# Two wide units for the last image's depthwise conv, and edge zeros stored one by one

## The chip, the core and the metric

The kernel runs on one core of a Trainium2 chip. The metric is the device time of one launch in microseconds; the time given is the median of three runs, and one further execution was taken with a profile. The engines are TensorE (PE, with its weight loads as PEld), VectorE (DVE), ScalarE (ACT), GpSimd (POOL) and SyncE (SP); SP, ACT and POOL also issue DMA transfers.

## What is computed

Input is x of 4 images, 128 channels, 128 x 128 pixels, all f32. Two layers follow each other. The first is a transformer-like block on overlapping 16 x 16 regions and the second a quantised residual block:

```
reg  = 9 x 9 regions of 16 x 16 pixels, step 14          # per image
y    = layernorm(tok); q, k, v = split(y @ w_qkv)        # 4 heads of 32
tok  = softmax(q k^T / sqrt(32)) v @ w_out + b_out + tok
xf   = overlapping regions added, divided by their count
y    = layernorm(xf) @ w_p0 + b_p0                       # 256 channels
ym   = depthwise 5 x 5 conv of y, padding 2, channel by channel
ym   = batchnorm over all images and pixels
x1   = gelu(gelu(ym)) @ w_p2 + b_p2 + xf

out  = conv3x3(act_quant(x1), weight_quant(w1)) -> batchnorm
out  = conv3x3(act_quant(out), weight_quant(w2)) -> batchnorm
result = out + x1
```

The batch norm after the depthwise conv needs the mean and variance of every channel over all four images. Nothing of the gelu stage can be computed before the last image's depthwise conv is done.

## The kernel before

**Bands.** The first layer goes through 36 bands, `bands[t] = (image, row of regions)`, nine a image. Band t has nine regions j = 0 to 8. For each region the loop at L1014 to L1027 issues the scores, the values of the region before, and four lists of side steps, which `beside(t)` (L917) lays out: the layer norm and q, k projections of later bands (`a1`, `a2`, from `ln1_chunks`), and for band t-1 the output projection, layer norm and the projection to 256 channels (`b1`, `b2`, from `post_chunks`). Of the eleven steps of a `b` chunk, 0 and 1 are the output projection, 2 to 6 the layer norm, and 7 to 10 the p0 projections, whose results `y` are stored to `y2_d` in DRAM. PE, ACT, DVE and SP execute in the order in which the code issues; POOL's order is the scheduler's.

**The depthwise conv.** It reads `y2_d` back with rows on the partitions: 16 output rows need 20 input rows of even and odd pixels, so 40 partitions. A group is 16 rows of an image, eight groups an image. Weights are banded matrices `dw_d`, made on the chip at the start. A unit, `units` at L170, is (image, first group, number of groups). One conv piece takes 8 channels of each of two halves; its matmuls (`depthwise`, L614) have 40 rows, 32 columns and 64 pixels x groups of moving columns. Images 0 to 2 are one unit of eight groups each; the last image is cut in three units of 4, 2 and 2 groups.

`conv_steps(n)` (L637) makes a list of steps for a unit: a begin that loads two tiles ahead, and then for each tile a step that loads the tile two ahead, does the matmuls into a `pm` bank, copies them with ACT to `c`, takes `bn_stats` with DVE, and puts the stores of `c` to `cv_d` in the list `stores`. `run` (L980) issues after each step the stores that were waiting before it. For the last image a tile has 640 KB of input in runs of 2 KB, 240 KB of weights, and 512 KB of results in runs of 256 bytes.

**When they run.** `todo` holds the waiting conv steps, `share` over how many bands they are spread. In `beside` (L925 to L935) an image's unit is queued two bands after its last band; for the last image the unit of four groups is queued in band 33 and spread over two bands, and the second unit goes into band 35 alone, with two pieces at a region (`twice`, lists `c` and `d`). A band takes `n` steps (L938) at the regions named at L953.

**The tail.** After the last band the pool context `bctx` is closed, with the conv's buffers `up` and `cp`. `conv_rest` (L715) opens new ones for the third unit: it loads all its weights with POOL (L609) and some input rows with SP at once; then the last band's projections run (`beside(T)`, L943 to L947); then `rest()` loads the missing rows and does eight steps of 16 channels, two groups wide, into the banks of the scores (`sc`), with `chunk_stats` after each. Then follow the batch norm (from L1097) and the gelu stage.

**The start.** The padding of `y2_d` must be zero. `band_matrices` (L213) makes a list of steps that also goes through `todo`, ten bands long: `zeros`, four steps `edges(b)` (for images 0 to 2 three stores of 256, 896 and 896 KB each from one zero tile, for the last image two of 256 KB), `padded_taps`, sixteen steps `by_outputs`, and the turning of the weights. For the bands up to 9 the lists are laid out anew at L973 to L977.

Of the kernel before, what the change touches and what calls it, by code (L numbers as in the profile page):

```python
# [8 lines left out]
F32 = mybir.dt.float32  # L9
# [5 lines left out]
P = 128  # L15
# [4 lines left out]
NR = (P - RS) // STEP + 1  # L20
NT = RS * RS
# [10 lines left out]
GR = 16  # L32
CW = P // 2
KD = 2 * (GR + 4)
NCK = 8
NG = P // GR + 1
# [12 lines left out]
def layers(  # L49
# [120 lines left out]
    units = [(b, 0, P // GR) for b in range(B - 1)] + [(B - 1, g, n) for g, n in ((0, 4), (4, 2), (6, 2))]  # L170
# [14 lines left out]
    with ExitStack() as actx:  # L185
# [7 lines left out]
        small = pool("small", 6)  # L193
        ps_s, ps_o, ps_m = (pool(n, k, space=PSUM) for n, k in (("ps_s", 1), ("ps_o", 1), ("ps_m", 3)))
# [5 lines left out]
        up, cp = pool("up", 3), pool("cp", 3)  # L200
# [12 lines left out]
        def band_matrices():  # L213
# [18 lines left out]
            def edges(b):  # L232
                if b == B - 1:
                    for d in (y2_d[b][0:2], y2_d[b][P + 2 :]):
                        nc.sync.dma_start(
                            out=d.rearrange("r e c x -> (r e c x)").rearrange("(p n) -> p n", p=P),
                            in_=held["zero"][:, : 8 * CW],
                        )
                    return
                for m, n, g in ((0, 8, 0), (4, 28, NG - 1), (18, 28, NG - 1)):  # L240
                    nc.sync.dma_start(
                        out=bass.AP(
                            y2_d[b].tensor, y2_d[b][m, 0, g, 0:1].offset,
                            [[n * NG * CW, P], [NG * CW, n], [1, CW]],
                        ),
                        in_=held["zero"][:, : n * CW].rearrange("p (n x) -> p n x", x=CW),
                    )

# [48 lines left out]
            steps = [zeros, *each(edges, [(b,) for b in range(B)]), padded_taps, lambda: None]  # L297
            steps += each(by_outputs, [(ro,) for ro in range(GR)])
# [338 lines left out]
        def conv_steps(n, ahead=2):  # L637
# [39 lines left out]
            def products(at):  # L677
                k, jj, c0 = tiles[at]
                ut, wt = U.pop(at), W[k, jj]
                pc = [ps_m.tile([P, nj, ng, CW], F32, name="pm") for _ in range(2)]  # L680
                depthwise(pc, wt[:, :, c0:], ut, nc_)
                for half in range(2):
                    cv = cp.tile([P, nj, ng, CW], F32, name="c")
                    nc.scalar.copy(  # L684
                        cv.rearrange("p j g x -> p (j g x)"), pc[half].rearrange("p j g x -> p (j g x)")
                    )
                    for j in range(nj):
                        nc.vector.bn_stats(  # L688
                            st0[:, k, half, 2 * jj + c0 // 4 + j, n, :], cv[:, j].rearrange("p g x -> p (g x)")
                        )  # L690
                        ch = 32 * k + 16 * half + 8 * jj + c0 + 4 * j
                        store(
                            bass.AP(
                                cv_d[b].tensor,
                                cv_d[b][g0, ch, 0:1].offset,
                                [[CW, P], [2 * P * GR * P, ng], [1, CW]],
                            ),
                            cv[:, j],
                        )
# [6 lines left out]
            for at in range(len(tiles)):  # L706
                def one(at=at):
                    if at + ahead < len(tiles):
                        load(at + ahead)
                    products(at)  # L710

                steps.append(one)
            return steps

        def conv_rest(n, w_t, u_t, c_t):  # L715

            b, g0, ng = units[n]
            early = 3  # L720
            at = GR + 2

            def load(k, a, z, g, m):
                for half in range(2):
                    ch = 32 * k + 16 * half
                    nc.sync.dma_start(
                        out=U[k][64 * half + 2 * a : 64 * half + 2 * z, g : g + m].rearrange(
                            "p g c x -> p g (c x)"
                        ),
                        in_=input_of(b, g0 + g, m, ch, 16, a, z),  # L730
                    )

            U = [u_t.tile([P, ng, 16, CW], F32, name=f"u{k}") for k in range(NCK)]
            W = [w_t.tile([P, 3, 16, 32], F32, name=f"w{k}") for k in range(NCK)]
            for k in range(NCK):
                weights(W[k], k, 0, 2, nc.gpsimd.dma_start)
            for k in range(early):
                load(k, 0, at, 0, 1)

            def late(k):  # L740
                if k < early:
                    load(k, 0, at, 1, 1)
                    load(k, at, GR + 4, 0, ng)
                else:
                    load(k, 0, GR, 0, ng)
                    load(k, GR, GR + 4, 0, ng)

            def step(k):
                sc = ps_s.tile([P, 2, 2, NT], F32, name=f"sc{k % 2}")
                pc = [  # L750
                    sc[:, half].rearrange("p a n -> p (a n)").rearrange("p (j g x) -> p j g x", j=4, g=ng)
                    for half in range(2)
                ]
                depthwise(pc, W[k], U[k], 16)
                for half in range(2):
                    cv = c_t.tile([P, 4, ng, CW], F32, name=f"c{half}")
                    nc.scalar.copy(
                        cv.rearrange("p j g x -> p (j g x)"), pc[half].rearrange("p j g x -> p (j g x)")
                    )
                    for j in range(4):  # L760
                        nc.vector.bn_stats(
                            st0[:, k, half, j, n, :], cv[:, j].rearrange("p g x -> p (g x)")
                        )
                    engine = (nc.sync, nc.scalar)[half]
                    for g in range(ng):
                        engine.dma_start(
                            out=bass.AP(
                                cv_d[b].tensor,
                                cv_d[b][g0 + g, 32 * k + 16 * half, 0:1].offset,
                                [[CW, P], [4 * GR * P, 4], [1, CW]],  # L770
                            ),
                            in_=cv[:, :, g],
                        )

            def run_all():
                for k in range(4):
                    late(k)
                for k in range(NCK):
                    step(k)
                    chunk_stats(k)  # L780
                    if k + 4 < NCK:
                        late(k + 4)

            return run_all
# [132 lines left out]
        def beside(t, sel=None):  # L917
# [7 lines left out]
            if t >= 2:  # L925
                b, i = bands[t - 2]
                if i == NR - 1 and b < B - 1:
                    todo.extend(conv_steps(b))
                    share[0] = NR if b < B - 2 else 5
                elif b == B - 1 and i == 4:  # L930
                    todo.extend(conv_steps(B - 1))
                    share[0] = 2
                elif b == B - 1 and i == 6:
                    todo.extend(conv_steps(B))
                    share[0] = 1  # L935
# [3 lines left out]
            conv = [todo.pop(0) for _ in range(n)]  # L939
# [3 lines left out]
            if t == T:  # L943
                return [
                    *conv, *left, *b1[:2], *b2[:2], b1[2], b1[3], b2[2], b2[3], b1[4], b2[4], b1[5], b2[5],
                    b1[6], *b1[7:], b2[6], *b2[7:],
                ]  # L947
# [3 lines left out]
            d = [[] for _ in range(NR)]  # L951
            twice = len(conv) > NR
            for j in sorted((1, 3, 5, 7, 8, 4, 6, 2, 0)[: len(conv)]):  # L953
                c[j] = [conv.pop(0)]
                d[j] = [conv.pop(0)] if twice and j and conv else []
# [17 lines left out]
            if t <= NR:  # L973

                left[:] = [*b1[9:], *b2[7:]]
                full = (f[:3], f[3:], b1[:2], a1[5:7], a1[7:], b2[:2], a2[5:7], a2[7:], b1[7:9])
                plan = [(one, two, w, four) for (one, two, three, four), w in zip(plan, full)]  # L977
            return [(one, two, three, four + d[j]) for j, (one, two, three, four) in enumerate(plan)]
# [9 lines left out]
        todo, share, left, early = [], [0], [], []  # L988
# [14 lines left out]
        with nullcontext() if safe else tc.manual_schedule(engines=MANUAL):  # L1003
# [25 lines left out]
            assert not todo  # L1029
# [4 lines left out]
            pools = [actx.enter_context(tc.tile_pool(name=f"late{n}_{tag}", bufs=n)) for n in (1, 2)]  # L1034
# [3 lines left out]
            rest = conv_rest(len(units) - 1, pools[0], pools[0], pools[1])  # L1038
            run(beside(T, selector(pools[0].tile([P, 4 * P], F32, name="sel"))))
# [403 lines left out]
```

## Time and profile before

| what | us |
|---|---|
| median of 3 runs (3217.94 to 3236.64) | 3229.64 |
| the profiled execution | 3224.37 |
| its span, first to last instruction | 3222.6 |
| PE busy in it (94%) | 3034.8 |
| DVE busy (63%) | 2018.5 |
| ACT busy (62%) | 1983.9 |
| POOL busy (26%) | 841.0 |

The bands begin, by the first matmul of their scores, at these times of the span:

| stretch | us of the span | length, us |
|---|---|---|
| band 2 | 117.0 to 178.0 | 61.0 |
| bands 3 to 8, each | from 178.0 | 47.6 to 48.5 |
| band 10, the first with conv | 514.8 to 581.5 | 66.7 |
| bands 20 to 26, each | from 1092.1 | 56.1 to 58.1 |
| bands 28 to 32, each | from 1547.8 | 68.5 to 73.2 |
| bands 33, 34, 35 | 1899.2 to 2193.3 | 84.2, 96.2, 113.7 |
| tail up to the batch norm's first matmul | 2193.3 to 2286.2 | 92.9 |

The page cuts the span in 40 slices of 80.6 us; a digit is the busy share in tenths, and PEclk the clock that TensorE was granted:

```profile
PE   8989998999999999999899998876899999999998
PEclk9999999999999999999999999977799999999999
GB/s 89 147 198 164 180 180 184 192 219 207 212 218 165 200 209 216 201 213 193 172 227 235 225 190 202 200 167 197 278 357 354 361 359 298 158 165 77 119 357 308
```

The columns 25 to 28 hold bands 33 to 35 and the tail. From column 29 on the gelu stage and the two 3 x 3 convs run, with PE above 90%.

The queues of the page, by packets, MB and share of the time of 16 DMA engines: q1 is issued by SP, q10 by ACT, q0 by POOL.

```profile
q1 hardware_dynamic: 763311, 645.37, 71.9%
q10 hardware_dynamic: 15712, 37.02, 4.4%
q0 software_dynamic: 1024, 3.93, 0.4%
```

### The profile page before, as it was taken

How to read it: one execution, taken by the hardware profiler on the slowest of the kernel's cores; microseconds unless marked ns; L12 is line 12 of the kernel's file. 1: busy time of each engine (PE TensorE's matmuls, PEld its weight loads, DVE VectorE, ACT ScalarE, POOL GpSimd, SP SyncE). 2: the span in 40 equal slices, each digit the busy share in tenths (PEclk: the TensorE clock that was granted, in tenths of full speed). 3: DMA queues.
4: the chain of work that ended last, by engine and by line, in shares of the span. 5: the costliest groups of instructions: out<-in, count | busy, mean ns of one | idle time of the engine just before them, and what ended most of it. 6: DMA issues, size and time to landing. Idle time of an engine off the chain costs nothing.

```text
span 3222.6 us, 92155 instructions
## 1 busy us (share of the span) xinstructions
PE 3034.8 (94%) x39162; PEld 1471.6 (46%) x39162; DVE 2018.5 (63%) x3244; ACT 1983.9 (62%) x2658; POOL 841.0 (26%) x1058
## 2 busy tenths in 40 slices
PE   8989998999999999999899998876899999999998
PEld 4545544444444444444444444454544444444443
DVE  5767886777776677767566654543555555666543
ACT  5767776777777777777666654532477777433433
POOL 3434443333333333333233231211111111000000
PEclk9999999999999999999999999977799999999999
DMA  3575777798886888887799978867899999442398
GB/s 89 147 198 164 180 180 184 192 219 207 212 218 165 200 209 216 201 213 193 172 227 235 225 190 202 200 167 197 278 357 354 361 359 298 158 165 77 119 357 308
DMA packets 780468, 692.32 MB, mean 215 GB/s; under 512 B 606022, under 2 KB 659599, under 8 KB 772367
## 3 DMA queue, kind: packets, MB, share of 16 engines
q1 hardware_dynamic: 763311, 645.37, 71.9%
q10 hardware_dynamic: 15712, 37.02, 4.4%
q8 instruction: 311, 5.10, 0.7%
q0 software_dynamic: 1024, 3.93, 0.4%
q14 instruction: 110, 0.90, 0.1%
HBM read 414.61 MB, written 275.51 MB: 214 GB/s over the span
## 4 chain that ended last, share of the span: by engine, by line
PE 73%; DMA 10%; ACT 6%; issue 4%; DVE 3%; SPq 3%; ACTq 0%; POOL 0%; DVEq 0%; POOLq 0%
PE pc L1200 21%; PE pm L448 16%; PE sc L820 8%; PE po L883 8%; PE pm L623 7%; PE pb L1264 6%; PE po L891 3%; DMA cv_d<-c 3%; PE pm L387 3%; ACT pt L828 2%; DMA y_d<-y 2%; DMA w<-dw_d 2%; DVE rd L903 1%; DMA xn<-row 1%; DMA row<-rstd 1%
## 5 line engine op out<-in xcount | busy, mean ns | idle before, releaser
L903 DVE RECIPROCAL rd<-po 128x256 f32<-128x256 f32 x324 | 568.6, 1755 | 372.7 <-PE po L891 371.7
L1200 PE MATMUL pc<-q,wq 128*128 128x512 fp8e4 x3168 | 699.4, 380 | 5.1 <-DVE q L1212 5.1
L828 ACT ACTIVATE pt<-sc 128x1024 f32<-128x1024 f32 x648 | 628.1, 1025 | 112.3 <-PE sc L820 55.1
L838 POOL TENSOR_TENSOR sm<-pt 128x512 f32<-128x512 f32 x324 | 415.4, 1282 | 1040.2 <-ACT pt L828 791.2
L1200 PEld LDWEIGHTS <-wq 128*128 128x128 fp8e4 x3168 | 308.8, 98 | 406.0 <-issue 37.3
L820 PE MATMUL sc<-q,kr 32*128 32x256 f32 x5184 | 402.3, 408 | 22.2 <-ACT pt L828 20.1
L623 PE MATMUL pm<-u,w 40*32 40x504 f32 (+5 forms) x7680 | 358.0, 497 | 27.1 <-DMA u<-y_d 16.9
L883 PE MATMUL po<-pt,v 128*32 128x256 f32 x5184 | 359.7, 395 | 17.3 <-DVE part L907 14.6
L820 PEld LDWEIGHTS sc<-q,kr 32*128 32x128 f32 x5184 | 248.0, 186 | 276.6 <-issue 177.6
L684 ACT COPY c<-pm 128x512 f32<-128x512 f32 (+1 forms) x256 | 133.7, 563 | 312.0 <-PE pm L623 177.7
L688 DVE BATCH_NORM_STATS2 st<-c 128x6 f32<-128x512 f32 (+2 forms) x320 | 162.5, 551 | 210.9 <-ACT c L684 210.8
L838 DVE TENSOR_TENSOR sm<-pt 128x512 f32<-128x512 f32 x324 | 245.0, 756 | 29.6 <-ACT pt L828 29.5
L448 PE MATMUL pm<-xn,wp 128*32 128x512 f32 (+1 forms) x2304 | 244.0, 549 | 17.3 <-ACT y L577 8.5
L448 PE MATMUL pm<-xn,wqkv 128*32 128x512 f32 (+1 forms) x2304 | 247.1, 551 | 7.7 <-ACT v L811 5.5
L577 ACT ACTIVATE y<-pm,vectors 128x512 f32<-128x512 f32 (+1 forms) x288 | 183.0, 643 | 106.9 <-DMA y_d<-y 53.2
L1264 PE MATMUL pb<-cv,wp 128*128 128x512 f32 x512 | 233.3, 599 | 4.7 <-ACT cv L1255 4.6
L623 PEld LDWEIGHTS pm<-u,w 40*32 40x32 f32 x7680 | 143.4, 111 | 202.3 <-issue 144.2
L883 PEld LDWEIGHTS po<-pt,v 128*32 128x32 f32 x5184 | 139.2, 111 | 187.4 <-issue 103.2
L1208 DVE BATCH_NORM_STATS2 st<-pc 128x6 f32<-128x512 f32 x256 | 165.8, 690 | 83.7 <-PE pc L1200 83.7
L891 PE MATMUL po<-sm,ones 128*32 128x256 f32 x2592 | 206.9, 388 | 0.1
L910 POOL TENSOR_TENSOR ob<-ob,part 128x32 f32<-128x32 f32 x288 | 127.3, 442 | 237.8 <-DVE part L907 230.2
L448 PE MATMUL pm<-wqkv,yr 128*32 128x128 f32 x5184 | 179.8, 278 | 0.0
(157 smaller groups left out, 3400.5 us busy)
## 6 DMA issues: line engine op xcount, KB each, us to landing
cv<-cv_d SPq DMA_DIRECT2D x64, 1024.0 KB
cv_d<-c SPq DMA_DIRECT2D x192, 256.0 KB
xn<-row SPq DMA_DIRECT2D x76, 512.0 KB
y_d<-y SPq DMA_DIRECT2D x142, 256.0 KB
xfl<-xf_d SPq DMA_DIRECT2D x64, 512.0 KB
id_d<-y SPq DMA_DIRECT2D x64, 512.0 KB
idt<-id_d SPq DMA_DIRECT2D x64, 512.0 KB
out_dram<-z SPq DMA_DIRECT2D x64, 512.0 KB
```

The lines of the kernel that those rows point to most:

```text
L448: nc.tensor.matmul(out[m], w[:, m], v, start=True, stop=True)
L577: nc.scalar.activation(y[:, :n], pm[:, : n * P].rearrange("p (r c e) -> p r e c", r=n, e=2), AF.Identity, bias=bp0[:, h : h + 1],)
L623: nc.tensor.matmul(outs[half][32 * q : 32 * q + 32, j, :, a:z], wt[hs, s, c, :], ut[hs, :, c, a + s - 1 : z + s - 1], start=(s == 1), stop ...
L820: nc.tensor.matmul(sc[h // 2][:, h % 2, kc, :].rearrange("p (r c) -> p r c", c=RS), region(kr, j)[hs, kc * P : (kc + 1) * P], queries(j, h ...
L828: nc.scalar.activation(pt, sc[p], AF.Exp)
L838: add(sm, pt[:, :, 0, :], pt[:, :, 1, :], ALU.add)
L883: nc.tensor.matmul(po[hs, 0, :], v[:, kc, hs], pt[h // 2][:, h % 2, kc, :], start=(kc == 0), stop=(kc == 1),)
L891: nc.tensor.matmul(po[hs, 1, :], ones, sm[h // 2][:, h % 2, :], start=True, stop=True)
L903: nc.vector.reciprocal(rd, po[:, 1, :])
L1200: nc.tensor.matmul(pc[:, h], w[:, t, :], q1[b][:, r + dy : r + dy + RB, dx : dx + P], start=(t == 0), stop=(t == 8),)
L1208: nc.vector.bn_stats(st[:, 2 * n + h, :], pc[:, h])
L1264: nc.tensor.matmul(pb[:, m], wp2[:, h, :], cv[:, h, px], start=(h == 0), stop=(h == 1))
```

## The change

The last image's conv is cut in two units of four groups. The first is queued in band 33 as before, but `share` is 7: bands 33, 34 and 35 take 2, 3 and 3 of its 17 steps, and what is left runs in the tail between the steps of the last projections. There it uses the score banks, and its copies, statistics and stores (`results`) come at the next piece (`pending`). `conv_rest` does the second unit in 16 pieces of 8 channels, with a ring of six inputs and weights; one half of each input is loaded by SP, the other by POOL. `up` and `cp` stay open in the tail.

The edge zeros become eleven single steps, one beside each of the first eleven `by_outputs`. The regions at which conv steps stand are chosen in another order when a list is fresh, and in the bands up to 9 the output projection of `b2` comes two regions earlier.

```diff
-    units = [(b, 0, P // GR) for b in range(B - 1)] + [(B - 1, g, n) for g, n in ((0, 4), (4, 2), (6, 2))]
+    units = [(b, 0, P // GR) for b in range(B - 1)] + [(B - 1, 0, 4), (B - 1, 4, 4)]
...
-            steps = [zeros, *each(edges, [(b,) for b in range(B)]), padded_taps, lambda: None]
-            steps += each(by_outputs, [(ro,) for ro in range(GR)])
+            steps = [zeros, padded_taps, lambda: None]
+            edges = [(b, m, n, g) for b in range(B - 1) for m, n, g in ((0, 8, 0), (4, 28, NG - 1), (18, 28, NG - 1))]
+            edges += [(B - 1, 0, 8, 0), (B - 1, 0, 8, 1)]
+            for ro in range(GR):
+                steps.append(several(*each(edge, edges[ro : ro + 1]), lambda ro=ro: by_outputs(ro)))
...
             def products(at):
                 k, jj, c0 = tiles[at]
                 ut, wt = U.pop(at), W[k, jj]
-                pc = [ps_m.tile([P, nj, ng, CW], F32, name="pm") for _ in range(2)]
+                if tail:
+                    pc = score_banks(at, ng)
+                else:
+                    pc = [ps_m.tile([P, nj, ng, CW], F32, name="pm") for _ in range(2)]
                 depthwise(pc, wt[:, :, c0:], ut, nc_)
+                return pc
...
                     if at + ahead < len(tiles):
                         load(at + ahead)
-                    products(at)
+                    while pending:
+                        pending.pop(0)()
+                    pc = products(at)
+                    if tail:
+                        pending.append(lambda: results(at, pc))
+                    else:
+                        results(at, pc)
...
+            tiles = [(k, jj) for k in range(NCK) for jj in range(2)]
+            ahead = 6
...
+            def load(at, a, z, g, m):
+                k, jj = tiles[at]
+                for half, engine in enumerate((nc.sync, nc.gpsimd)):
+                    engine.dma_start(
+                        out=U[at][64 * half + 2 * a : 64 * half + 2 * z, g : g + m].rearrange(
                             "p g c x -> p g (c x)"
                         ),
+                        in_=input_of(b, g0 + g, m, 32 * k + 16 * half + 8 * jj, 8, a, z),
                     )
...
+            for at in range(ahead):
+                begin(at)
+                load(at, 0, GR, 0, ng - 1)
+                load(at, GR, GR + 4, 0, ng - 2)
...
             def run_all():
+                for at in range(ahead):
+                    load(at, 0, GR, ng - 1, 1)
+                    load(at, GR, GR + 4, ng - 2, 2)
+                for at in range(len(tiles)):
+                    step(at)
+                    if at % 2:
+                        chunk_stats(at // 2)
+                    if at + ahead < len(tiles):
+                        begin(at + ahead)
+                        load(at + ahead, 0, GR, 0, ng)
+                        load(at + ahead, GR, GR + 4, 0, ng)
...
                     todo.extend(conv_steps(B - 1))
-                    share[0] = 2
-                elif b == B - 1 and i == 6:
-                    todo.extend(conv_steps(B))
-                    share[0] = 1
+                    share[0] = 7
...
             if t == T:
+                more = lambda n: [todo.pop(0) for _ in range(min(n, len(todo)))]
                 return [
-                    *conv, *left, *b1[:2], *b2[:2], b1[2], b1[3], b2[2], b2[3], b1[4], b2[4], b1[5], b2[5],
-                    b1[6], *b1[7:], b2[6], *b2[7:],
+                    *more(2), *b1[:2], *b2[:2], b1[2], *more(1), b1[3], b2[2], *more(1), b2[3], b1[4], b2[4],
+                    *more(1), b1[5], b2[5], *more(1), b1[6], *b1[7:], b2[6], *more(1), *b2[7:], *more(len(todo)),
                 ]
...
-            for j in sorted((1, 3, 5, 7, 8, 4, 6, 2, 0)[: len(conv)]):
+            order = (1, 5, 7, 3, 8, 4, 6, 2, 0) if fresh else (1, 5, 3, 7, 8, 4, 6, 2, 0)
+            for j in sorted(order[: len(conv)]):
...
-                full = (f[:3], f[3:], b1[:2], a1[5:7], a1[7:], b2[:2], a2[5:7], a2[7:], b1[7:9])
+                full = (f[:3], f[3:], b1[:2], b2[:2], a1[5:7], a1[7:], a2[5:7], a2[7:], b1[7:9])
...
             run(left)
             left.clear()
             flush(len(stores))
-            rest = conv_rest(len(units) - 1, pools[0], pools[0], pools[1])
-            run(beside(T, selector(pools[0].tile([P, 4 * P], F32, name="sel"))))
+            rest = conv_rest(len(units) - 1, late)
+            run(beside(T, selector(late.tile([P, 4 * P], F32, name="sel"))))
+            run(pending)
             flush(len(stores))
             rest()
```

## The prediction

> **What bounds the kernel now.** I read the windows by stage first, cut where a band's first scores start. Columns: stretch, its length, busy time of PE, weight loads, DVE, ACT, POOL with counts, granted clock, DMA share, GB/s.
>
> ```profile
> core 0: us, PE busy (x) PEld busy (x) DVE busy (x) ACT busy (x) POOL busy (x), PEclk, DMA share, GB/s
> ...
> 1092.10:1490.20 398.10, 392.79 (x6396) 185.67 (x6392) 283.40 (x440) 289.70 (x439) 147.12 (x186) 1.00 0.87 209
> 1899.20:1983.40 84.20, 73.08 (x1408) 39.41 (x1400) 45.65 (x81) 44.72 (x69) 21.11 (x27) 0.92 0.81 186
> 1983.40:2079.60 96.20, 79.91 (x1600) 43.54 (x1592) 48.68 (x91) 46.66 (x73) 19.90 (x24) 0.93 0.87 204
> 2079.60:2193.30 113.70, 88.14 (x2232) 54.37 (x2224) 48.46 (x116) 42.19 (x77) 17.26 (x20) 0.82 0.65 171
> 2193.30:2233.80 40.50, 20.07 (x144) 7.19 (x144) 8.22 (x15) 10.00 (x17) 10.12 (x20) 0.79 0.86 231
> 2233.80:2286.20 52.40, 43.27 (x1536) 39.73 (x1537) 26.02 (x133) 8.59 (x16) 0.00 (x0) 0.50 0.69 166
> 2338.00:2528.00 190.00, 190.00 (x675) 84.75 (x674) 104.24 (x156) 134.15 (x105) 27.07 (x26) 1.00 0.99 358
> ```
>
> Bands 20 to 26 (the first row) are bound by PE: 393 of 398 us at full clock, 57 us a band. Bands 33, 34, 35 take 84, 96 and 114 us for the same attention, with gaps on PE and a clock below one. The tail is 40.5 us up to the first matmul of `conv_rest` and 52.4 us from there to the batch norm; its second half runs at 0.50 although PE is 83% busy. The last row is the gelu stage, for the rate that long-run transfers reach.
>
> Then PE's timeline, for what one conv piece costs (start, duration, instruction, records; an fp32 matmul leaves two records):
>
> ```profile
> 1920.20 5.29 PE L623 MATMUL pm<-u,w 40*32 40x256 f32 x88 [1.87 <-DMA u<-y_d]
> 1930.16 2.79 PE L623 MATMUL pm<-u,w 40*32 40x256 f32 x96
> 2002.12 5.77 PE L623 MATMUL pm<-u,w 40*32 40x256 f32 x96 [2.39 <-ACT y L577]
> 2233.84 20.33 PE L623 MATMUL sc<-u,w 40*32 40x128 f32 x738 [7.38 <-DMA u<-y_d]
> ```
>
> A piece of the four-group unit (256 columns) is 2.8 us at full clock and 5.8 at half. Neither 5.8 us of such matmuls nor the 47 us of `conv_rest` brought the clock back; it rose once scores and values followed.
>
> Last, who waited in bands 33 to 35 (total us, times, longest):
>
> ```profile
> ACT c L684 <- DMA cv_d<-c: 74.7, 23, 7.2
> PE pm L623 <- DMA u<-y_d: 16.9, 7, 4.7
> ```
>
> Result buffers and loads both wait for transfers: the conv pieces put in there are paced by DMA, and ACT, which must also feed the attention, waits with them.
>
> At the other end, band 2 (117 to 178 us) takes 61 us where bands 4 to 8 take 48. SP's timeline, and a wait of PE in it:
>
> ```profile
> 142.90 8.09 SPq L241 DMA_DIRECT2D y_d<-u  x3
> ...
> 155.05 6.60 SPq L241 DMA_DIRECT2D y_d<-u  x3
> 161.75 3.46 SPq L421 DMA_DIRECT2D xn<-row  x1
> 165.26 6.70 SPq L241 DMA_DIRECT2D y_d<-u  x3
> ```
>
> ```profile
> PE po L883 <- DVE part L907: 12.3, 2, 10.0
> ```
>
> Three edge stores go out at a time (2.1 MB: 256, 896 and 896 KB), and the `xn<-row` load that the layer norm needs stands behind them; DVE waits for it, and PE for DVE.
>
> **What the skill says.** (1) "TensorE: Matmul & The Clock Gate", Part 1: the clock is half or full only, set by an activity window of about 3.4 us, and falls after an idle window. The trace agrees (0.50 and 1.00; gaps of 3.5 to 4.7 us in band 35 are followed by 0.50). The page does not say that a busy but narrow matmul stream fails to release the clock; the fence above shows it. (2) "DMA: Bandwidth & Descriptors", Specifications: transfers under 512 B miss line rate. The trace agrees: windows full of 256-byte runs (results, y, edges) move about 222 GB/s for a full DMA share (198 at 0.89 from 130 to 165 us), the gelu stage 358. (3) The same page, "Issuing engines are not separate DMA queues": a second issuing engine saves only issue time. So moving half of `conv_rest`'s loads to POOL buys no bandwidth; the weight loads that POOL issues before take a median 11.0 us to land, in the list of DMA issues.
>
> **Part by part**, against the profiled run's 3224.4 us (span 3222.6; the median of the runs, 3229.6, is 0.16% above it).
>
> *Bands 33 to 35.* Before: 2193.3 - 1899.2 = 294.1 us with 7, 9 and 16 pieces, the first and last band with a begin besides. After: `share` 7 gives 17//7 = 2 (begin and one piece), then 3, then 3. A band without conv: bands 20 to 26 hold 1296 conv records of 512 columns at 58 ns (48 in 2.78 us at 547 us) = 75 us, so (393 - 75)/7 = 45.4 us of PE a band. Band 33: 45.4 + 2.8; band 34: 45.4 + 8.4; band 35: 45.4 + 8.4 - 7.7, since it has no next band's layer norm and projections (6.1 and 1.6 us of PE). Sum 148.1. I add 5 us a band for waits: band 32, with six wide pieces, has 6.2 us of gaps. That is 163, and 131 less than before. DMA doesn't stop it: band 34 needs some 10.6 MB (6.4 of its own by the list of DMA issues, three pieces of 1.4), 183 GB/s.
>
> *Tail, first part.* Before: 40.5 us, PE 20.1 busy. Nine pieces come in. At full clock 9 x 2.8 = 25, at half 52; pieces and dense projections alternate, I take 4.3 us each, 39. The idle 20 us (waiting for POOL's seams, for y buffers) mostly goes under the pieces; 8 remain. That makes 67. Transfers: 9 results of 0.5 MB, y and xf 3.9 MB, 7 loads of 0.64, weights, and the early loads of `conv_rest` (12 on SP, 24 with weights on POOL, 4.2 MB) that SP must issue first at 0.76 us each, ahead of the pieces' own loads and stores. That is about 68 us at full DMA share, 79 at the 0.86 of this window. I take 75. The 12 loads on POOL wait for y rows; `post_begin` could stand behind them, about 5 us, under the first two pieces.
>
> *Tail, second part.* The first matmul waits 7.4 us in before for the last y store and the load after it. Now the two last pieces lie there, but SP issues the late loads only behind those pieces' result stores, so I keep 7.4. Then 16 pieces of 256 columns instead of 8 steps of 2 x 128: at half clock 16 x 5.8 = 92 against 47.3. Copies (2 x 0.59), statistics and issues of a piece stay under 4 us, hidden. End 5.1 as before. Sum 105, for 52.4 + 7.4 inside the old tail.
>
> Tail: 75 + 105 = 180 for 92.9, so +87. Its 40 MB need 71 us for 15.7 MB of short runs and 68 for the rest, 139 at full share: PE at half clock is the bound, not DMA.
>
> *Bytes.* One unit less saves 16 weight loads of 0.24 MB, 3.9 MB, inside the above; so are 768 fewer narrow matmuls, since time goes with columns.
>
> *Start.* Edges in pieces: the three-store step becomes single stores, one beside each `by_outputs`. Band 2 loses its 13 us. Not all is gained: band 3 gets six edges, 4.2 MB, 19 us of DMA on a share of 0.61 x 48 = 29, so it is full; I give 4 us back there, 1 in band 4, and 2 in band 2, where the taps' load still holds SP (9.2 us). Gain 6; ends 0 (all waits move on) and 12.
>
> *Order.* First pieces at regions 1, 5, 7 instead of 1, 3, 5 in bands 10 and 19, and a projection of the band before two regions earlier in bands 1 to 9: PE gaps there sum to 7.4 us in bands 3 to 8, and the two long ones of band 10 come from the begin's loads, which stay. I take 2; ends -2 and 8. Keeping `up` and `cp` open costs no instruction.
>
> Sum: -131 + 87 - 6 - 2 = -52: 3224.4 - 52 = 3172.
>
> **Rivals.**
> *The clock comes back* (or stays up): wider matmuls have a smaller share of weight loads, and one window nearly full of them in band 33 (2.9 us from 1947.6) kept 1.00. Against: from cold, the 5.3 and 5.8 us of them in the fence did not release it. Then the tail is bound by transfers, 155 us: 3224 - 131 + 62 - 8 = 3147.
> *The tail's transfers bind at its present mean rate*: 18 MB in 92.9 us is 194 GB/s; 40 MB take 206 us: 3224 - 131 + 113 - 8 = 3198. For it: three result buffers instead of four, landings of 5 to 7 us. Against: six loads ahead.
> *Slower than before*: the tail overlaps as badly as `conv_rest` alone does now. Place: SP's queue there, where loads stand behind results waiting for ACT. Price: at its 166 GB/s, 40 MB are 241 us, 148 more than before: 3224 - 131 + 148 - 8 = 3233, and 3242 at 160. It decides once the tail passes 232 us, below 172 GB/s. Against it: two issuing engines for the loads, and attention is no longer in the queue.
>
> **How the numbers follow.** Forecast 0.50 (own range 3150 to 3190); clock comes back 0.20; mean rate 0.18; slower case 0.12. One measurement of this kernel tells about 0.5% (16 us) from no change. Faster by more: 0.50 + 0.20 + 0.15 of the mean-rate case = 0.85; within: 0.03 + 0.04 of the slower case = 0.07; slower by more: 0.08. The range for 8 in 10 leaves out the slower case and the fast end of the clock case: 3125 to 3212.
>
> **What would show it.** Right: bands 33 to 35 of 50 to 60 us; a tail near 180 us with 0.50 in its second part and 5.8 us a piece; band 2 near 50. Wrong: bands 33 to 35 still above 65 us, a tail over 230 us, or pieces of 2.8 us there.

## The result, and the profile after

The changed kernel takes 3232.89 us in the median of 12 runs, the kernel before 3230.64: a ratio of 1.0006 with a 95% interval of 0.9995 to 1.0018. Nothing that can be measured has changed in the time, and nearly everything has changed in its parts. The stages of the two profiled executions, in us, cut at the first scores of each band, at the end of attention, at the second unit's first matmul and at the batch norm's:

| stage | before | after | forecast |
|---|---|---|---|
| up to band 2 | 117.0 | 114.1 | |
| bands 2, 3, 4 | 61.0, 48.5, 47.9 | 52.7, 58.3, 62.0 | 6 less in all |
| bands 5 to 9 | 240.3 | 232.5 | 2 less, with bands 1 to 4, 10 and 19 |
| bands 10 to 32 | 1384.4 | 1383.4 | |
| bands 33, 34, 35 | 84.2, 96.2, 113.7 | 52.7, 54.9, 52.8 | 163 in all |
| tail, first part | 40.5 | 106.4 | 82 |
| tail, second part | 52.4 | 116.2 | 97 |
| from the batch norm on | 936.4 | 937.4 | |

The three bands give 133.7 us and the tail takes 129.7; the start loses 15.6 in bands 2 to 4 and gains 7.8 in bands 5 to 9 and 2.9 before. The windows of the changed kernel answer to those of the kernel before, with the same columns:

```profile
core 0: us, PE busy (x) PEld busy (x) DVE busy (x) ACT busy (x) POOL busy (x), PEclk, DMA share, GB/s
1903.10:1955.80 52.70, 50.10 (x831) 26.64 (x827) 37.65 (x61) 39.03 (x58) 20.70 (x27) 1.00 0.74 186
1955.80:2010.70 54.90, 54.04 (x1020) 29.30 (x1016) 39.39 (x68) 40.44 (x61) 19.97 (x24) 1.00 0.72 181
2010.70:2063.50 52.80, 51.23 (x976) 28.53 (x976) 37.31 (x61) 33.88 (x48) 17.31 (x20) 0.97 0.73 186
2063.50:2169.90 106.40, 59.11 (x1021) 31.54 (x1014) 20.90 (x51) 20.89 (x37) 23.36 (x40) 0.66 0.91 192
2169.90:2286.10 116.20, 85.36 (x1536) 60.23 (x1536) 33.93 (x133) 17.66 (x32) 24.39 (x40) 0.50 0.76 157
```

The bands are bound by PE again: 95% busy or more at nearly full clock, with a quarter of the DMA engines' time to spare. In the tail neither is full: PE is busy for 59 of 106 and 85 of 116 us, and the DMA share is 0.91 in the first part and only 0.76 in the second. PE's timeline tells what a piece waits for (start, duration, records, and in brackets the idle time before and what ended it):

```profile
2069.43 3.64 PE L447 MATMUL pm<-ob,wo 128*32 128x512 f32 x32
2094.25 1.08 PE L622 MATMUL sc<-u,w 40*32 40x256 f32 x8 [21.18 <-DMA u<-y_d]
2099.60 5.29 PE L622 MATMUL sc<-u,w 40*32 40x256 f32 x88 [4.27 <-DMA u<-y_d]
...
2188.85 5.41 PE L622 MATMUL sc<-ur,wr 40*32 40x256 f32 x96 [3.30 <-ACT c L769]
2197.96 5.42 PE L622 MATMUL sc<-ur,wr 40*32 40x256 f32 x96 [3.70 <-ACT c L769]
```

At the head of the tail PE stands 21 us, then 4, for the first unit's third piece. In the second part a piece's matmuls take 5.4 us at half clock, but many have a gap of 1 to 4 us before them, until ACT has copied a result out of the score bank. What ACT waits for is in the list of waits over the tail (total us, times, longest):

```profile
ACT c L690 <- DMA cv_d<-c: 62.1, 9, 33.7
ACT c L769 <- DMA cv_d<-c: 61.3, 12, 7.3
```

A copy needs one of three `c` buffers, and a buffer comes free when its store has landed. L769 is the second unit's copy, L690 the first unit's.

At the start, SP's timeline of band 3 has single edge stores (L241) with the stores of the banded matrices (L254) and the layer norm's load behind them, and the waits of bands 3 and 4 show the price:

```profile
204.07 1.14 SPq L241 DMA_DIRECT2D y_d<-u  x1
205.25 3.12 SPq L254 DMA_DIRECT2D band_d<-pad_d  x2
208.41 0.56 SPq L420 DMA_DIRECT2D xn<-row  x1
210.53 0.56 SPq L241 DMA_DIRECT2D y_d<-u  x1
211.14 6.82 SPq L254 DMA_DIRECT2D band_d<-pad_d  x2
218.07 0.38 SPq L420 DMA_DIRECT2D xn<-row  x1
```

```profile
DVE xn L430 <- DMA xn<-row: 23.8, 4, 10.8
...
PE po L897 <- DVE part L921: 19.9, 3, 9.8
```

The `xn` load issued at 208.4 stands behind an edge and two band stores; DVE could start on it only at 216.0, after a wait of 10.8 us. PE has a gap of 9.8 us in band 3 and one of 9.3 in band 4, and at each of them the granted clock drops to half for 10.2 us.

### The profile page after: what moved, and what is told of

Read it like the earlier page. It is cut to its first block, busy times and chain, and to the rows that moved or that the text cites. A ratio compares the mean times of both kernels' runs of the same rounds, so it can differ in the third digit from the quotient of the medians.

```text
span 3223.5 us, 88862 instructions
## 1 busy us (share of the span) xinstructions
PE 3023.7 (94%) x37626; PEld 1465.0 (45%) x37626; DVE 2009.6 (62%) x3180; ACT 1983.7 (62%) x2642; POOL 876.8 (27%) x1118
## 4 chain that ended last, share of the span: by engine, by line
PE 74%; DMA 11%; ACT 5%; DVE 4%; issue 3%; SPq 1%; ACTq 1%; POOL 0%; DVEq 0%; POOLq 0%
PE pc L1211 21%; PE pm L447 17%; PE sc L834 8%; PE po L897 8%; PE pm L622 7%; PE pb L1275 7%; DMA cv_d<-c 4%; PE po L905 3%; PE pm L386 3%; DMA y_d<-y 2%; DMA xn<-row 2%; ACT pt L842 2%; DVE rd L917 2%; DMA u<-y_d 1%; PE sc L622 1%
## 5 line engine op out<-in xcount | busy, mean ns | idle before, releaser
L622 PE MATMUL pm<-u,w 40*32 40x504 f32 (+3 forms) x5280 | 287.5, 562 | 0.8 <-DMA u<-y_d 0.8
L694 DVE BATCH_NORM_STATS2 st<-c 128x6 f32<-128x512 f32 (+1 forms) x256 | 147.0, 617 | 165.7 <-ACT c L690 165.3
L690 ACT COPY c<-pm 128x512 f32<-128x512 f32 x206 | 111.4, 591 | 183.7 <-PE pm L622 142.4
L1283 DVE SCALAR_TENSOR_TENSOR y<-pb,vectors,xfl 128x512 f32<-128x512 f32 x128 | 90.3, 747 | 139.7 <-PE pb L1275 127.4
```

The costliest lines, as they stand in the source:

```text
L622: nc.tensor.matmul(outs[half][32 * q : 32 * q + 32, j, :, a:z], wt[hs, s, c, :], ut[hs, :, c, a + s - 1 : z + s - 1], start=(s == 1), stop ...
```

## The experiments

All edits are to the changed kernel unless said otherwise. Stage lengths come from one profile each and are set beside those of the changed kernel; bands 10 to 32, which no edit touches, took 1383 to 1399 us in these profiles, so single total times say little, and the kernel before took 3250.5, 3243.5 (median of 7) and 3243.6 beside the three groups of runs. Stages differ between profiles too where the code is the same. The tail took 222.6 us in the changed kernel and 227.1 in its run with the edges back, 92.9 in the kernel before and 98.2 with one early line changed; bands 33 to 35 took 294.1 and 307.1 in that last pair. A difference of 5 us in the tail therefore says nothing.

**Edges back in one step per image.**

```diff
-            for ro in range(GR):
-                steps.append(several(*each(edge, edges[ro : ro + 1]), lambda ro=ro: by_outputs(ro)))
+            steps[1:1] = [several(*each(edge, [e for e in edges if e[0] == b])) for b in range(B)]
+            steps += each(by_outputs, [(ro,) for ro in range(GR)])
```

> The changed kernel with the edge zeros again in one step per image (three stores at a time), all else as changed. Theory (each single edge store, and the band stores beside it, stands ahead of one xn load on SP, so ten waits replace a few): bands 2, 3, 4 go back from 53, 58 and 62 us to about 61, 48 and 48, so 16 us less, and bands 5 to 9 stay at 46 to 47. Rival (bands 3 and 4 lose by the earlier output projection or the other regions of the steps, not by the edges): bands 3 and 4 stay near 60 us.

Its windows, band 2, 3 and 4:

```profile
122.70:186.30 63.60, 49.34 (x736) 25.88 (x732) 36.53 (x59) 36.75 (x55) 21.61 (x28) 0.87 0.87 199
186.30:232.10 45.80, 45.52 (x735) 24.17 (x732) 34.30 (x53) 36.64 (x55) 19.99 (x26) 1.00 0.59 177
232.10:278.80 46.70, 45.66 (x731) 23.86 (x728) 36.04 (x56) 36.86 (x55) 20.47 (x27) 1.00 0.56 169
```

156.1 us against 173.0: bands 3 and 4 are back below 47, and bands 5 to 9 stay at 231.7. In these bands the single edge stores lose 17 us; the rival falls. Bunched, the stores spoil one band; spread, they delay a load in each of two. Not all of it is gained in the end: the stretch up to band 2 took 122.7 us here and 114.1 in the changed kernel (116.4 to 120.6 in other profiles with the same start). From the first scores to band 5 the bunched stores take 251.8 us, the single ones 260.7 to 268.1 in seven profiles, so they lose 9 to 16. Whether a load is late by its place in SP's queue or because the DMA engines have no time is not shown. Over the changed kernel's bands 3 and 4 their share is 0.71 and 0.69, which speaks for the queue; around the late load, from 199 to 217 us, it is 0.85.

**Eight result buffers in the tail.**

```diff
-                    cv = cp.tile([P, nj, ng, CW], F32, name="c")
+                    cv = tail[0]() if tail else cp.tile([P, nj, ng, CW], F32, name="c")
...
-                    cv = cp.tile([P, 2, ng, CW], F32, name="c")
+                    cv = tail[0]()
...
-            tail.append(True)
+            tail.append(lambda: late.tile([P, 2, 4, CW], F32, name="cl", bufs=8))
```

> The changed kernel with eight result buffers for the conv pieces of the tail instead of three. Theory (ACT's copies wait for results to land, since three buffers hold one piece and a half): the second part of the tail falls from 116 us to about 95, 5.6 us a piece, and the first part by up to 10. Rival (the DMA engines' rate is the bound there): pieces stay near 7 us, the landings only take longer, and the tail stays within 5 us of 223.

The tail's two parts, then ACT's wait for landings in the second:

```profile
2080.90:2185.40 104.50, 58.32 (x1024) 28.69 (x1021) 20.70 (x52) 21.42 (x38) 23.61 (x40) 0.68 0.93 199
2185.40:2272.80 87.40, 82.21 (x1537) 74.72 (x1537) 33.66 (x133) 17.20 (x32) 24.48 (x40) 0.50 0.96 204
```

```profile
ACT cl L769 <- DMA cv_d<-cl: 8.1, 2, 4.1
```

PE's timeline in the second part:

```profile
2185.37 61.58 PE L622 MATMUL sc<-ur,wr 40*32 40x256 f32 x1152 [10.43 <-DMA ur<-y_d]
2247.44 20.62 PE L622 MATMUL sc<-ur,wr 40*32 40x256 f32 x384 [0.49 <-DMA ur<-y_d]
```

The second part falls by 28.8 us, the wait from 61.3 to 8.1 us, and the matmuls are 94% of the time. So the three buffers cost those 29 us. PE now works through the sixteen pieces with one gap of 0.5 us: in this part the forecast's bound, PE at half clock, is reached. The first part hardly moves (-2): ACT's waits had held PE for only 7.4 us there (gaps of 1.4, 3.0 and 3.1), and other gaps took their place. And the DMA share is now 0.96 at 204 GB/s: with the wait for buffers gone, PE at half clock and the DMA engines reach their end together.

**The early loads in the middle of the projections.**

```diff
-            rest = conv_rest(len(units) - 1, late)
-            run(beside(T, selector(late.tile([P, 4 * P], F32, name="sel"))))
+            rest = []
+            plan = beside(T, selector(late.tile([P, 4 * P], F32, name="sel")))
+            plan.insert(18, lambda: rest.append(conv_rest(len(units) - 1, late)))
+            run(plan)
```

> The changed kernel with the early loads of the second unit issued in the middle of the last projections (after their fourth conv piece but one) instead of ahead of all of them. Theory (they stand ahead of the third piece's load on SP and on the DMA engines): the gaps of 21 and 4 us on PE before the third and fourth piece go, and the first part of the tail falls from 106 us to about 85. Rival (the same bytes have to pass in any order): the gap reappears later, at the start of the second part, and the tail gains less than 8 us.

The first part took 106.2 us, as before the edit; the gap before the third piece shrank to 2.8 and 1.7 us, and one of 12.5 appeared before the fourth, another of 8.9 in the layer norm. The tail as a whole took 219.1 us, 3.5 less, within the 8 us of the rival. But the edit did less than it says. SP's twelve loads moved to 2141 us, but POOL's order is the scheduler's, and POOL still issued its 24 loads at once, as the queues of its first 28 us show (q0 is POOL's: packets, MB, share of the engines):

```profile
q1 hardware_dynamic: 6946, 3.22, 59.0%
q0 software_dynamic: 1034, 2.13, 42.7%
```

So it leaves the question open; the run without the early loads takes it up again.

**The first unit in bands 33 to 35 alone.**

```diff
-                    share[0] = 7
+                    share[0] = 3
```

> The changed kernel with the first unit spread over bands 33 to 35 alone (4, 6 and 6 pieces and a begin), none of it in the tail. Theory (a piece costs 2.8 us of PE beside attention, at full clock and with transfers hidden, and over 8 us in the tail): the three bands take about 62, 67 and 65 us, 34 more than changed; the tail's first part falls from 106 to about 45; 25 us less in all. Rival (pieces are paced by transfers wherever they stand, as in bands 33 and 34 of the kernel before): the bands take 75 us and more each and the sum stays within 8 us.

The three bands, then the tail's two parts:

```profile
1919.40:2121.60 202.20, 187.70 (x3677) 103.03 (x3672) 127.51 (x224) 120.81 (x183) 58.83 (x71) 0.96 0.84 197
2121.60:2164.60 43.00, 20.53 (x156) 7.33 (x157) 8.35 (x16) 12.31 (x20) 19.02 (x32) 0.77 0.94 222
2164.60:2275.10 110.50, 85.74 (x1537) 55.03 (x1537) 33.89 (x133) 17.66 (x32) 28.68 (x49) 0.50 0.83 172
```

Nine pieces moved from the tail to the bands: the bands grow by 41.8 us, 4.6 a piece, and the tail's first part shrinks by 63.4, 7.0 a piece. With 5.7 off the second part, the stages are 27 us shorter together, as the theory said; a piece in a band cost more than its 2.8 us, though. Band 34 took 74.4 us, and PE's two long gaps in it wait for ACT:

```profile
1987.23 0.64 PE L386 MATMUL pm<-sq,ones 128*32 128x256 f32 x8 [3.87 <-ACT sq L380]
2000.66 0.70 PE L834 MATMUL sc<-q,kr 32*128 32x256 f32 x4 [2.42 <-ACT pt L842]
```

ACT had waited for stores to land just before:

```profile
1985.64 0.58 ACT L690 COPY c<-pm 128x512 f32<-128x512 f32 x1 [4.59 <-DMA cv_d<-c]
1997.55 0.58 ACT L576 ACTIVATE y<-pm,vectors 128x384 f32<-128x384 f32 x1 [4.49 <-DMA y_d<-y]
```

So transfers are not free beside attention either.

**Both.** The edits of the last run and of the eight buffers.

> The changed kernel with both: the first unit in bands 33 to 35 alone, and eight result buffers in the tail. Theory (the two losses lie in different stages and add up): bands 33 to 35 about 202 us as with the spreading alone, the tail's parts about 43 and 87 us, so 332 from band 33 to the batch norm where changed has 383: about 50 us less, 3182. Rival (both only relieve the same transfers): together they gain no more than 35 us.

Bands 203.0, tail 44.0 and 92.0: 339 us, 44 less than the changed kernel and 7 short of what was expected, above the rival's 35. So the two gains (30.8 and 27.3 us in these stages) add up to three quarters. The median of four runs is 3201.86 us beside 3243.47 of the kernel before: 0.9874, interval 0.984 to 0.9907.

**Both, and the edges from POOL.**

```diff
-                nc.sync.dma_start(
+                nc.gpsimd.dma_start(
                     out=out, in_=held["zero"][:, : n * CW].rearrange("p (n x) -> p n x", x=CW)
                 )
```

> As the kernel with both, and the single edge stores issued by POOL instead of SP. Theory (an edge store costs by standing ahead of an xn load in SP's queue): bands 2 to 4 fall from 175 us to about 150, so 25 us less again, about 3157. Rival (the DMA engines' time is what is short there, whichever engine issues): bands 2 to 4 stay above 168 us.

Bands 2, 3 and 4:

```profile
128.50:180.60 52.10, 47.84 (x732) 24.93 (x729) 37.04 (x59) 36.64 (x55) 21.03 (x27) 0.93 0.53 133
180.60:227.20 46.60, 45.39 (x732) 24.16 (x728) 36.17 (x56) 36.64 (x55) 20.47 (x27) 1.00 0.51 152
227.20:274.00 46.80, 45.75 (x732) 24.06 (x728) 35.84 (x56) 36.77 (x55) 20.49 (x27) 1.00 0.58 171
```

145.5 us against 173.8 with both. But POOL, free in its order, sent all eleven stores from 59 to 93 us, in bands 0 and 1, which took 12 us longer (46.5 and 55.0 against 42.7 and 46.9). From the first scores to band 5 it takes 247.1 us, 16 less than with both, where bunching gave 9 to 16. Since the stores moved in time as well as to another queue, this run doesn't tell the two apart. The median is 3178.33 us, ratio 0.9802 to the kernel before, interval 0.9779 to 0.9824: it beats the kernel before, and so the changed kernel, which took 1.0006 of it.

**Dense matmuls to raise the clock**, on top of the eight buffers. Their results are read by nobody.

```diff
+                for _ in range(10 if at == 0 else 1):
+                    nc.tensor.matmul(pd[:, :384], ident, wqkv, start=True, stop=True)
                 depthwise(pc, W[at], U[at], 8)
```

> The changed kernel with eight result buffers, and dense matmuls added whose results nobody reads: ten of 128 x 128 x 384 before the second unit and one before each of its pieces. Theory (a narrow stream does not release the clock, and with eight buffers the DMA engines are full, over 0.9): the clock comes up in the second part and a piece's matmuls take 2.8 us, but the part stays at 78 us or more, 9 less than with the buffers alone at best. Rival (the half clock is the bound there): it falls to 16 x 3.5 = 56 us and about 15 around it, near 70.

PE's timeline at the start of the second part:

```profile
2167.51 8.24 PE L767 MATMUL po<-wqkv,ident 128*128 128x384 f32 x20
2177.55 3.18 PE L622 MATMUL sc<-ur,wr 40*32 40x256 f32 x96 [1.80 <-DMA ur<-y_d]
...
2181.51 2.79 PE L622 MATMUL sc<-ur,wr 40*32 40x256 f32 x96
2184.23 0.91 PE L767 MATMUL po<-wqkv,ident 128*128 128x384 f32 x2
2185.07 2.79 PE L622 MATMUL sc<-ur,wr 40*32 40x256 f32 x96
...
2194.44 1.08 PE L622 MATMUL sc<-ur,wr 40*32 40x252 f32 x13 [3.06 <-issue]
2195.45 1.65 PE L767 MATMUL po<-wqkv,ident 128*128 128x384 f32 x2
2197.03 5.32 PE L622 MATMUL sc<-ur,wr 40*32 40x256 f32 x96
```

The burst brought the clock up, and four pieces ran at 2.8 to 3.2 us, with a dense matmul of 0.9 us before all but the first; then PE stood 3.1 us and went on at half clock to the end, without a gap and with the dense matmuls as pure load (1.65 us in every 7). The second part took 104.6 us. That is above the 78 us of the theory, but not for its reason, since the clock stayed up for four pieces only; the rival's 70 was not met either. The 3.1 us don't look like a wait for a load: they fall within a piece, after 83 of its 96 records, and the profile names nothing that ended them. A 16 KB packet of an instruction queue passed in that time, which is no proof that PE waited for it. So this run shows that the clock can be brought up, and leaves open why it was lost and what a part wholly at full clock would take.

**Without the early loads**, on top of the eight buffers.

```diff
-            for at in range(ahead):
-                begin(at)
-                load(at, 0, GR, 0, ng - 1)
-                load(at, GR, GR + 4, 0, ng - 2)
...
-                    load(at, 0, GR, ng - 1, 1)
-                    load(at, GR, GR + 4, ng - 2, 2)
+                    begin(at)
+                    load(at, 0, GR, 0, ng)
+                    load(at, GR, GR + 4, 0, ng)
```

> The changed kernel with eight result buffers and without the second unit's early loads: all its inputs and weights are loaded after the first unit's last piece. Theory (with eight buffers the tail is bound by its bytes at the mixed rate of about 204 GB/s, and the order only moves a gap): the gaps of 23 and 4 us before the third and fourth piece go and the first part falls from 104 to about 80 us, but the second part has 4.2 MB more to load and grows from 87 to about 105, so that the sum stays within 6 us of 192. Rival (the early loads stand in the wrong place and that is all): the second part grows by 8 at most and the sum falls by 15 or more.

The tail's two parts, and PE's first matmul of the second:

```profile
2082.00:2178.90 96.90, 62.44 (x1020) 29.67 (x1016) 20.67 (x52) 21.42 (x38) 14.64 (x24) 0.68 0.94 198
2178.90:2283.20 104.30, 84.29 (x1536) 63.18 (x1537) 33.60 (x133) 17.28 (x32) 26.66 (x44) 0.50 0.96 187
```

```profile
2178.94 21.46 PE L622 MATMUL sc<-ur,wr 40*32 40x256 f32 x397 [18.01 <-DMA ur<-y_d]
```

The gap of 23 us before the third piece became one of 4.7, and one of 18.0 stands before the second part. The sum is 201.2 us against 191.9, so the rival (15 less) falls; the theory's 6 us are missed by 3, which is less than the spread between profiles. The early loads do make the gap at the head, but it can't be had for nothing: the DMA share is 0.94 and 0.96 throughout, and the same bytes cost the time elsewhere.

**The best kernel without the early loads**, the last edit on that kernel.

> The best kernel so far (first unit in bands 33 to 35, eight buffers, edges from POOL) without the early loads. Theory (early loads use time of the DMA engines that the projections leave, so they are worth their bytes): the second part grows from 90 to about 105 us and the first stays near 43, 12 to 15 us slower. Rival (the early loads hinder the projections' own stores): the first part falls below 38 us and the sum is no longer than 133.

First part 34.3 us instead of 43.1, second 105.7 instead of 90.3: 6.6 longer in all, between the two expectations. The rival had the first part right (below 38), the theory the second. The same tail with the loads took 136.0 us in the kernel with both and 133.4 in the best one, so the 140.0 here are 4 to 7 more, hardly above the spread: the loads are worth half of what was thought at most.

**One line of the change on the kernel before.**

```diff
-                full = (f[:3], f[3:], b1[:2], a1[5:7], a1[7:], b2[:2], a2[5:7], a2[7:], b1[7:9])
+                full = (f[:3], f[3:], b1[:2], b2[:2], a1[5:7], a1[7:], a2[5:7], a2[7:], b1[7:9])
```

> The kernel before with one line of the change: in bands 1 to 9 the output projection of the second chunk two regions earlier. Theory (this, and not the edges, shortens bands 5 to 9): they go from 240 to about 232 us, all else as before, 8 us less with band 1. Rival (the steps' other regions or the shorter list do it): no change above 2 us.

Bands 5 to 9 took 231.8 us against 240.3, and 3 and 4 took 46.5 and 46.8: the earlier projection is what shortens these bands, by 1.1 to 2.0 us each. PE over bands 5 to 9 before and with the line:

```profile
274.50:514.80 240.30, 233.93 (x3644) 119.27 (x3642) 201.46 (x299) 184.18 (x275) 109.79 (x132) 1.00 0.66 178
275.50:507.30 231.80, 228.45 (x3647) 120.71 (x3644) 200.82 (x299) 184.82 (x275) 110.05 (x132) 1.00 0.70 185
```

Only 3.0 of the 8.5 us were gaps on PE (6.4 and 3.4 us); the other 5.5 are busy time of nearly the same count of records, at the same clock. Why they take less is not shown.

## Why the prediction was wrong

The forecast was 52 us less; the spans say 1 us more. By its own terms:

- *Bands 33 to 35* (163 us): right, 160.4. PE's content plus some waits was the sum to make, and transfers didn't stop it.
- *Tail, first part* (75, and 7.4 of wait): 106.4. The step that failed is its transfer sum, "about 68 us at full DMA share, 79 at the 0.86 of this window". Measured, the share was 0.91 over 106 us, so 97 us of the engines' time, for 20.6 MB. The early loads were counted in issue time on SP and in bytes, but the third piece's load behind them was not followed to its landing: 25 us of PE gap. Leaving them out closes most of that gap, but shortens the part by only 7.6 us (104.5 to 96.9, both with eight buffers), so the order is the smaller step, and the transfers' sum, 97 for 68, the larger. The wait before the second part was 8.7 us for 7.4.
- *Tail, second part* (92 and 5.1): 116.2. The matmuls were as forecast, at half clock throughout (5.4 us a piece for 5.8). What was "hidden" (copies, statistics and issues of a piece) was not: three buffers hold one and a half pieces, and landing put 29 us in, as the eight buffers showed. The prediction named the buffers, but as evidence for a rival instead of a term with a price: four buffers before, three after, over pieces with the same 0.5 MB of results. What a full clock would have been worth here stays open.
- *"PE at half clock is the bound, not DMA"*: with enough buffers this holds for the second part, but not for the first. The floor of 139 us took 358 GB/s for the long runs, from a stage that only has 4 KB packets. With eight buffers and a share of 0.93 and 0.96 the tail still needed 192 us, at 199 and 204 GB/s, for its 38.6 MB. The bytes were right (40 forecast), the rate was not: 38.6 MB at 212 GB/s, about those rates at full share, are 182 us, where the forecast had 139. It is the long runs that were slow. In the first part of the changed kernel's tail the 256-byte packets passed at 217 GB/s, counted over 16 engines, close to the 222 assumed, but SP's 2 KB packets at 204 and POOL's 4 KB packets at 195, where 358 was assumed. Packets overlap (the share is 1.04 from 2073.0 to 2099.6 us), so a packet's time includes waiting beside others. The rival with the mean rate (206) and the slower one (above 232) lie on both sides of the measured 222.6; buffers and rate made it together, where the prediction had them apart.
- *Start* (6 less): 15.6 more in bands 2 to 4. Band 2 gained 8 of 13. The failed step is the price in band 3, "so it is full; I give 4 us back there, 1 in band 4": the band's DMA share was 0.71, and bands 3 and 4 lost 24 us, because the stores ahead of an `xn` load made it late and PE then stood nearly 10 us in each of them. With the edges back in one step the 24 us are gone; whether the queue's order or the engines' time makes the load late stays open.
- *Order* (2 less, ends -2 and 8): 7.8 less in bands 5 to 9, all from the earlier projection. The failed step is that only gaps on PE were counted (7.4 us in six bands): most of what fell away was PE's busy time, as the one-line run shows.

Summed against the forecast: the tail 43 us too low, the start 22, against 6 from the order, 3 from bands 33 to 35 and 3 before band 2; that is the 53 us between the forecast and the result. The change does take the conv out of the way of the attention, and the time comes back where the attention no longer hides its transfers: in the tail nine more pieces cost 7 us each where beside attention they cost 4.6.

## What to carry to other kernels

Work moved from a full stage to an empty one takes its transfers along: before pricing it by the engine, divide its bytes by the rate that a mixed stage of that kernel has reached, and count how many results its buffers hold against the time that a store takes to land. A store can cost more by what stands behind it than by its bytes: ask of each store in a queue which load stands next behind it, and whether spreading the stores lets them delay more loads. The best version here (0.9802 of the time before) keeps the wide units, puts the pieces back beside the attention, has more result buffers, and issues the edges from POOL.

## What the hardware showed

- A stream of matmuls of 40 rows and 32 columns didn't bring the clock from half to full: with eight buffers 61.6 us of it without a gap stayed at 0.50. Once at full clock it kept it for 5.4 us on its own (two pieces at the head of the changed kernel's tail, 192 records from 2064.14 us), and through four pieces with a dense matmul before all but the first, after a burst of ten. In the last case the clock fell after a 3.1 us gap, and one dense fp32 matmul in each 7 us didn't bring it back in the 82 us that followed.
- The DMA engines at a share of 0.96 moved 204 GB/s in a mix of 256-byte stores and loads in 2 and 4 KB packets, beside 358 GB/s at 0.99 in the gelu stage.
